# Local attention: eight masked maxima of one head each on VectorE in place of two mask products on TensorE and two maxima

## The chip, the cores and the metric

The kernel runs on one core of a Trainium2 chip. A core has TensorE (PE in the profile; PEld is its loading of weights), VectorE (DVE), ScalarE (ACT), GpSimd (POOL) and a queue for transfers (SP), each with its own stream of instructions and with semaphores between them. SBUF is the working memory of 128 partitions; PSUM has eight banks of 2 KB a partition, which TensorE writes and VectorE and ScalarE read or write. The metric is the time of one execution in microseconds; the kernel before took 3221.06 us, the median of three runs (3219.2 to 3222.68).

## The reference

Four sequences of 1024 tokens with 128 features pass six layers in turn: a gated stack `ffn0`, an attention of 16 heads, `ffn0` again, a stack `ffn1`, an ordinary causal attention, and `ffn1` again. Only `ffn1` holds the change. It has two layers, each a local attention and a gated layer. Cut to the local attention (8 heads of 64, windows of 64 tokens):

```python
q = l2norm(q) * qs
k = l2norm(k) * ksc
q, k = rotary_xpos(q, k)
bq = q.reshape(b, h, w, WINDOW, d) * QK_SCALE
bk, bv = look_around(bk), look_around(bv)          # a window sees itself and the one before
sim = jnp.einsum('bhwid,bhwjd->bhwij', bq, bk)     # 64 queries against 128 keys
mask = (i < j) | (i > j + WINDOW) | (j == -1)
sim = jnp.where(mask, -jnp.finfo(sim.dtype).max, sim)
attn = jax.nn.softmax(sim, axis=-1)
out = jnp.einsum('bhwij,bhwjd->bhwid', attn, bv)
```

So every head's scores get the same mask, the maximum of each row is taken after the mask, and the softmax is exp(score + mask - maximum), divided by its sum.

## The kernel before, in words

The data stays in SBUF as eight blocks of 512 tokens, each of four tiles of 128 tokens: 32 tiles. In an `ffn1` phase `attend` runs once for each tile and layer, 64 times, and there are two such phases: 128 tiles in all. For one tile the steps are: the projections of queries, keys and values (`project`, TensorE); sums of squares (`square` on ScalarE, `sums` on VectorE); the rotary products (`turn_a`, `turn_b` on VectorE, `add` and `normalise` on GpSimd); transposes and their copies (`turn`, `untwist`); the scores (`score`); the maxima (`top`); the exponentials with their sums (`exp`, ScalarE); the reciprocals and the division (`inverse` on VectorE, `norm_e` on GpSimd); transposes and copies of the weights (`turn_e`, `untwist_e`); the product with the values, the output projection and its addition (`weigh`, `output`, `project_out`, `collect`). VectorE also takes the statistics of other tiles (`statistics`), a Newton step for the inverse roots (`newton`) and the low half of transposed inputs (`lower`).

The scores of a tile lie in two PSUM banks (numbers 6 and 7, tag `s`), z = 0 and 1, each 128 rows (two windows of 64 queries) by four heads by 128 keys. `score` first writes the mask into both banks: one product of the identity in bf16 with the mask `lm`, 128x512, which repeats the 128x128 mask four times. The 32 products of the heads are then added to it. `top` takes, in one reduction a bank, the four maxima with their sign turned, and `exp` runs once for each of the eight heads, with this column as its bias and its row sum taken on the way. The masks, one for tiles in the middle and one for the first tile of a sequence (n = 0), are loaded by `mask` on GpSimd's queue at the start of a phase.

The order of the work isn't that of the source. Steps are recorded with a nominal time (`at`); the table `OFF` gives each step's place within a tile and `T_ATT` the pitch from tile to tile, so some five tiles are under way at a time. The planner (`Plan`) then gives every instruction a cost (`cost`), and each step its buffers, and orders all steps of the whole program over the five engines by when they must be done (`order`, `latest`; the best of six rounds). The result is one fixed order for each engine; at run time each engine takes its instructions in that order and waits on semaphores. A change of one step's cost can so move any instruction, in other phases too. Every instruction is issued through one helper, so nearly all rows of the profile carry its line, L237; they are told apart by operation, shape and tiles. The gated layers (`gated`) run in groups of four or eight blocks between the tiles.

Of `OFF`, the places that matter here:

```python
"ghi": 19.08, "sc": 19.56, "glo": 20.34, "mx0": 23.03, "mx1": 23.63, "ex03": 24.03, "ex01": 24.38, "ex00": 25.76,
"ex13": 26.10, "ex11": 26.45, "ex10": 26.79, "ex12": 27.14, "ex02": 27.48, "iv1": 28.04, "ne1": 28.53,
```

`ex03` is the exponential of bank 0, head 3: of each bank, the last head's comes first.

## Time and profile before

| | |
|---|---|
| time of the runs | 3221.06 us (3219.2 to 3222.68) |
| the profiled execution's own time | 3219.6 us |
| its span, first to last instruction | 3217.8 us |
| mean granted clock of TensorE | 0.984 |
| busy: PE, PEld | 3029.4 us (94%), 2134.7 us (66%) |
| busy: DVE, ACT, POOL | 2192.4 us (68%), 2467.9 us (77%), 1451.3 us (45%) |
| the mask products, 128x512 bf16 | 230 recorded, 383 ns each |
| the maxima, 128x4 out of 128x512 | 256, 681 ns each |
| the exponentials and others of 128x128 on ACT | 1152, 392 ns each |

The page cuts the span into 40 slices of 80 us and gives the busy share of each engine in tenths. A row of instructions gives the engine, the operation, what is written and read, partitions by elements, the count, the busy time and the mean duration of one, and then the idle time of the engine before these, with what ended it. A matmul's record includes its way through the array, so the records of products that follow each other overlap; VectorE's records overlap by some 80 ns too. What an instruction costs its engine is therefore read from one start to the next. The timeline gives start, duration, engine, operation and count of successive instructions; the table of stretches gives each engine's busy time within them. The chain of waits is followed back from the last instruction and says in whose work the time lay. A few records of products are missing from the trace.

### The profile page before, as it was taken

Reading aid. Unit: us, or ns where it says so; the run is one execution under the profiler, and the core shown is the slowest. Engines: PE = TensorE matmul, PEld = TensorE weight load, DVE = VectorE, ACT = ScalarE, POOL = GpSimd, SP = SyncE. Lnnn points to the kernel's source line nnn. Section 1 sums busy time; section 2 is a strip of 40 time slices with the busy share of each in tenths; the row PEclk is TensorE's granted clock in tenths of the full one; section 3 lists DMA queues with packets and bytes.
Section 4 is the critical chain, followed back from the end, with each engine's and each line's share of the span. In section 5 each row is a group of like instructions: output and inputs, shape, how many; then the busy total and the mean of one; then the engine's idle time right before and its main releaser. Section 6 shows DMA issues by size and latency. Waiting matters only on the chain.

```text
span 3217.8 us, 76341 instructions
## 1 busy us (share of the span) xinstructions
PE 3029.4 (94%) x27082; PEld 2134.7 (66%) x27108; DVE 2192.4 (68%) x6641; ACT 2467.9 (77%) x6856; POOL 1451.3 (45%) x1621
## 2 busy tenths in 40 slices
PE   8999999989998999899999999999999899999978
PEld 6322222567776777677777777777777677777767
DVE  8433341467867676778788778878787777676774
ACT  6999999768868687657777777767777788686873
POOL 1000000079958585523333333333343898585870
PEclk9999999999999999899999999999999999999989
DMA  1000000022212221122222222212231322222211
GB/s 40 1 1 1 1 3 11 21 68 63 57 40 58 44 56 35 42 57 49 47 55 45 46 50 45 52 44 47 54 80 34 76 54 56 44 53 49 55 42 30
DMA packets 209427, 137.31 MB, mean 43 GB/s; under 512 B 148548, under 2 KB 164632, under 8 KB 209048
## 3 DMA queue, kind: packets, MB, share of 16 engines
q1 hardware_dynamic: 208328, 131.87, 18.1%
q8 instruction: 217, 3.56, 0.5%
q14 instruction: 162, 1.33, 0.1%
q0 software_dynamic: 720, 0.56, 0.1%
HBM read 17.58 MB, written 2.10 MB: 6 GB/s over the span
## 4 chain that ended last, share of the span: by engine, by line
PE 58%; ACT 16%; DVE 13%; issue 5%; POOL 5%; DMA 1%; SPq 1%; DVEq 0%; ACTq 0%; POOLq 0%
PE wordsP L237 58%; ACT wordsS L237 12%; DVE wordsS L237 8%; POOL wordsS L237 3%; ACT words L237 3%; DVE words L237 3%; POOL words L237 1%; SPq L237 1%; DVE wordsP L237 1%; DVE wordsR L237 1%; DMA wordsS<-wordsS 1%; ACT wordsR L237 0%; DMA words<-words 0%; ACT wordsP L237 0%; DMA wordsS<-L_attn_x 0%
## 5 line engine op out<-in xcount | busy, mean ns | idle before, releaser
L237 PE MATMUL wordsP<-wordsS 128*128 128x128 f32 (+8 forms) x12062 | 1657.9, 331 | 114.2 <-POOL wordsS L237 44.1
L237 ACT ACTIVATE wordsS<-wordsP,wordsS 128x128 f32<-128x128 f32 (+4 forms) x1952 | 921.6, 495 | 335.7 <-PE wordsP L237 204.1
L237 PEld LDWEIGHTS wordsP<-wordsS 128*128 128x128 f32 (+3 forms) x10296 | 926.0, 145 | 329.4 <-POOL wordsS L237 85.3
L237 POOL TENSOR_SCALAR wordsS<-wordsS 128x128 f32<-128x128 f32 (+7 forms) x630 | 476.1, 758 | 678.6 <-DVE wordsS L237 484.5
L237 PE MATMUL wordsP<-wordsR 128*128 128x512 f32 (+2 forms) x2592 | 718.9, 409 | 13.6 <-ACT words L237 4.1
L237 POOL TENSOR_TENSOR wordsS<-wordsS 128x512 f32<-128x512 f32 (+1 forms) x512 | 532.6, 1053 | 430.2 <-DVE wordsS L237 411.4
L237 ACT COPY wordsS<-wordsP 128x512 f32<-128x512 f32 (+4 forms) x1040 | 543.8, 541 | 170.6 <-PE wordsP L237 160.7
L237 DVE TENSOR_REDUCE wordsS<-wordsP 128x1 f32<-128x512 f32 (+4 forms) x1024 | 576.9, 582 | 70.6 <-PE wordsP L237 64.1
L237 PE MATMUL wordsP<-wordsS,words 128*64 128x64 f32 (+3 forms) x6216 | 524.0, 299 | 34.6 <-DVE words L237 12.6
L237 ACT ACTIVATE wordsS<-wordsP 128x1024 f32<-128x1024 f32 (+3 forms) x646 | 516.8, 863 | 27.1 <-PE wordsP L237 22.7
L237 PEld LDWEIGHTS wordsP<-wordsR 128*128 128x128 f32 (+1 forms) x2592 | 451.1, 191 | 115.2 <-ACT words L237 10.2
L237 PE MATMUL wordsP<-words 128*128 128x512 f32 (+3 forms) x1540 | 414.7, 375 | 13.0 <-DMA words<-W_vT 10.9
L237 ACT ACTIVATION_READ_ACCUMULATOR wordsS<-wordsP,wordsS 128x1 f32 x1792 | 397.2, 222 | 0.0
L237 DVE COPY wordsS<-wordsP 128x512 f32<-128x512 f32 (+4 forms) x444 | 238.8, 551 | 219.0 <-PE wordsP L237 213.5
L237 PEld LDWEIGHTS <-wordsS 64*128 64x128 bf16 (+1 forms) x1792 | 117.7, 95 | 390.3 <-issue 373.1
L237 PEld LDWEIGHTS wordsP<-wordsS,words 128*64 128x64 f32 (+2 forms) x5704 | 302.6, 136 | 101.5 <-issue 48.1
L237 DVE TENSOR_TENSOR wordsS<-wordsP,wordsS 128x256 f32<-128x256 f32 (+3 forms) x560 | 252.7, 463 | 161.5 <-PE wordsP L237 122.8
L237 DVE TENSOR_TENSOR words<-wordsP,wordsS 128x256 f32<-128x256 f32 (+1 forms) x448 | 227.8, 527 | 133.4 <-PE wordsP L237 87.9
L237 PEld LDWEIGHTS wordsP<-words 128*128 128x128 f32 x1540 | 247.6, 192 | 44.1 <-DMA words<-W_kT 10.9
L237 PEld LDWEIGHTS wordsP<-words,wordsS 64*64 64x64 f32 (+1 forms) x4672 | 186.8, 142 | 79.4 <-issue 54.3
L237 PE MATMUL wordsP<-words,wordsS 64*64 64x128 f32 (+1 forms) x4672 | 227.3, 279 | 8.0 <-POOL words L237 3.1
L237 ACT ACTIVATE words<-wordsP,wordsS 128x512 fp32r<-128x512 f32 (+1 forms) x192 | 131.0, 689 | 69.8 <-PE wordsP L237 67.9
(62 smaller groups left out, 2219.7 us busy)
## 6 DMA issues: line engine op xcount, KB each, us to landing
words<-words SPq DMA_DIRECT2D x648, 128.0 KB
wordsS<-words SPq DMA_DIRECT2D x88, 128.0 KB
wordsS<-wordsS SPq DMA_DIRECT2D x48, 128.0 KB
wordsS<-wordsS SPq DMA_DIRECT2D x48, 112.0 KB
wordsS<-c_rot SPq DMA_DIRECT2D x16, 256.0 KB
wordsS<-L_attn_x SPq DMA_DIRECT2D x8, 256.0 KB
words<-wordsS SPq DMA_DIRECT2D x16, 128.0 KB
out_dram<-wordsS SPq DMA_DIRECT2D x8, 256.0 KB
```

Source lines behind the costliest of these rows:

```text
L237: self.follow(engine, getattr(engine.engine, name)(*args, **kw))
```

## The change

The two mask products are left out, and the heads' products now start their own sums. `top` becomes four instructions a bank, eight a tile, on VectorE: each takes one head's 128x128 scores from PSUM, adds the 128x128 mask, turns the sign, writes the result back to the same place and keeps the minimum of each row, which is the maximum with its sign turned. `exp` reads the negated scores with a scale of -1. The mask tile is 128x128 in place of 128x512.

```diff
         def mask(k):
-            W["lm", k] = tile_([128, 512], f"lm{k}", 1, BF)
-            gp.dma_start(out=W["lm", k], in_=a["c_local"][k])
+            W["lm", k] = tile_([128, 128], f"lm{k}", 1, BF)
+            gp.dma_start(out=W["lm", k], in_=a["c_local"][k][:, 0:128])
...
             def score():
                 qT, kT = V["qT", K], V["kT", K]
                 scs = V["s", K] = [plan.bank(pre + "s", [6, 7], (128, 4, 128)) for _ in range(2)]
-                for sc in scs:
-                    pe.matmul(flat(sc), self.identb, W["lm", int(n == 0)], start=True, stop=False, skip_group_check=True)
...
-                                start=False,
+                                start=True,
                                 stop=True,
                                 skip_group_check=True,
...
             def top(z):
                 if z == 0:
                     V["m", K] = tile_([128, 8], "nm", 2), tile_([128, 8], "su", 2), tile_([128, 8], "rc", 2)
-                ve.tensor_reduce(V["m", K][0][:, 4 * z : 4 * z + 4], V["s", K][z], AX.X, ALU.max, negate=True)
+
+                for c in range(4):
+                    sc = lambda: V["s", K][z][:, c, :]
+                    ve.tensor_tensor_reduce(
+                        out=sc(), in0=sc(), in1=W["lm", int(n == 0)], scale=-1.0, scalar=-NEG,
+                        op0=ALU.add, op1=ALU.min, accum_out=V["m", K][0][:, 4 * z + c : 4 * z + c + 1],
+                    )
...
                 ac.activation(
                     V["e", z, K][:, c, :], V["s", K][z][:, c, :], AF.Exp,
-                    bias=nm[:, u : u + 1], accum_out=su[:, u : u + 1],
+                    bias=nm[:, u : u + 1], scale=-1.0, accum_out=su[:, u : u + 1],
                 )
```

## The prediction

> **What bounds the kernel now.** I read the page's slices first, to find the stages that the change touches. The two local-attention phases lie at about 683 to 1348 and 2505 to 3147 us of the span; the rest holds no edited instruction.
>
> ```profile
> PE   8999999989998999899999999999999899999978
> DVE  8433341467867676778788778878787777676774
> ```
>
> There TensorE is near full and VectorE at six to eight tenths, but a slice mixes attention with gated blocks. So I asked for the stretches in which one tile's row maxima follow the next at an even pitch, and for one stretch of gated work (904 to 940):
>
> ```profile
> core 0: us, PE busy (x) PEld busy (x) DVE busy (x) ACT busy (x) POOL busy (x), PEclk, DMA share, GB/s
> 697.00:904.00 207.00, 192.82 (x2329) 149.42 (x2333) 163.19 (x514) 176.50 (x662) 188.20 (x193) 0.99 0.26 58
> 904.00:940.00 36.00, 35.67 (x264) 29.77 (x266) 14.67 (x29) 18.60 (x43) 5.72 (x7) 0.99 0.11 22
> 941.00:1081.00 140.00, 127.14 (x1517) 98.28 (x1519) 108.86 (x326) 116.47 (x440) 117.36 (x119) 0.99 0.24 53
> 1117.00:1252.00 135.00, 126.85 (x1525) 100.26 (x1526) 104.33 (x320) 116.59 (x439) 114.58 (x115) 0.97 0.26 56
> 2524.00:2731.00 207.00, 192.64 (x2326) 149.76 (x2328) 161.38 (x512) 177.29 (x663) 186.83 (x191) 0.99 0.26 58
> 2766.00:2907.00 141.00, 128.01 (x1521) 99.42 (x1522) 109.39 (x326) 116.65 (x440) 117.87 (x120) 0.98 0.24 53
> 2943.00:3080.00 137.00, 127.07 (x1525) 100.28 (x1526) 105.47 (x322) 116.25 (x439) 116.55 (x118) 0.98 0.25 55
> ```
>
> Counted by their row maxima, the six attention stretches hold 23, 15, 15, 23, 15 and 15 tiles: 106 of the 128, in 967 us, 9.12 us a tile. Busy per tile: PE 894.5/106 = 8.44, POOL 841.4/106 = 7.94, ACT 819.8/106 = 7.73, DVE 752.6/106 = 7.10. Nothing is alone at the limit; DVE is the emptiest of the four, with 2.0 us a tile to spare. In the gated stretch DVE is 41% busy and no maximum is taken.
>
> The chain of waits agrees that the load is shared. For 697 to 904:
>
> ```profile
> by line: PE wordsP L237 48.0%; POOL wordsS L237 13.4%; ACT wordsS L237 10.2%; ACT words L237 8.1%; DVE wordsS L237 6.8%; issue 5.1%; POOL words L237 2.9%; DVE wordsP L237 2.4%; DVE words L237 1.7%; ACT wordsR L237 0.6%; DVE wordsR L237 0.5%
> ```
>
> DVE holds 11% there, PE 48%. The same line for the other five stretches, in order, gives PE 15, 34, 34, 12, 26% and DVE 28, 19, 18, 26, 23%: where PE holds less, DVE and ACT hold more. Last, who waits for DVE, in the first stretch:
>
> ```profile
> POOL wordsS L237 <- DVE wordsS L237: 15.1, 15, 2.7
> ```
>
> POOL, 91% busy there (188.2 of 207), has its longest waits on DVE.
>
> **Removed from PE.** Per tile, two mask products. In the timeline of PE:
>
> ```profile
> 1123.56 0.61 PE L237 MATMUL wordsP<-wordsS 128*128 128x512 bf16 x2
> 1124.09 1.10 PE L237 MATMUL wordsP<-words,wordsS 64*64 64x128 f32 x32
> ```
>
> The scores start 0.53 us after the masks: 0.53 us a tile, 68 us over 128 tiles as PE work. What of it sets the end goes by PE's share of the chain: 0.53/8.44 = 6.3% of PE's chain time, in the six stretches 6.3, 1.3, 2.9, 4.5, 1.1 and 2.3 us, together 18 us.
>
> **Removed from DVE.** Two reductions of 128x512, each followed 0.59 us later (the next instruction starts before the recorded end):
>
> ```profile
> 797.59 0.68 DVE L237 TENSOR_REDUCE wordsS<-wordsP 128x4 f32<-128x512 f32 x1
> 798.18 0.28 DVE L237 TENSOR_TENSOR wordsS<-wordsP,wordsS 128x128 f32<-128x128 f32 x1
> ```
>
> That is 1.18 us a tile.
>
> **Added to DVE.** The built order of VectorE shows that each of the eight new instructions becomes two: the 128x128 pass and a read-out of the accumulator into a 128x1 column. It also shows a wait that the diff does not: in every group of four, the second, third and fourth pass wait for VectorE's own semaphore, which the read-out before them raises. No such pair is in the trace; the nearest rows are these, where the statistics' second half waits in the same way for the first:
>
> ```profile
> 780.32 0.28 DVE L237 TENSOR_TENSOR wordsS<-wordsP,wordsS 128x128 f32<-128x128 f32 x1
> 780.52 0.18 DVE L237 TENSOR_SCALAR wordsP<-wordsP 128x18 f32<-128x18 f32 x1
> 780.60 0.29 DVE L237 BATCH_NORM_STATS2 wordsS<-wordsS 128x6 f32<-128x128 f32 x1
> 780.93 0.18 DVE L237 BATCH_NORM_AGGREGATE wordsS<-wordsS 128x2 f32<-128x6 f32 x1
> 781.02 0.26 DVE L237 BATCH_NORM_STATS2 wordsS<-wordsS 128x6 f32<-128x128 f32 x1
> ```
>
> The pass is priced as the 128x128 tensor-tensor from PSUM: next start 0.20 us after its own. The read-out has the size of the 128x1 operations, 0.15 us, and 0.06 until an unwaited follower. A follower that waits starts 0.04 us after the end (780.60 + 0.29 = 780.89, start 780.93). So one step is 0.20 + 0.15 + 0.04 = 0.39, a group 3 x 0.39 + 0.20 + 0.06 = 1.43, a tile 2.86; net +1.68 us of DVE a tile.
>
> Bounds: if the wait and the new kind of instruction cost nothing beyond these rows, 8 x 0.26 = 2.08, net +0.90. If the read-out cannot start before the pass has ended (0.28 + 0.04 + 0.15 + 0.04 = 0.51 a step), a tile is 2 x (3 x 0.51 + 0.38) = 3.82, net +2.64. I take the middle value because ScalarE's own pairs overlap in that way:
>
> ```profile
> 781.20 0.37 ACT L237 ACTIVATE wordsS<-wordsP,wordsS 128x128 f32<-128x128 f32 x1
> 781.45 0.21 ACT L237 ACTIVATION_READ_ACCUMULATOR wordsS<-wordsP,wordsS 128x1 f32 x1
> ```
>
> The read-out starts 0.25 us into a pass of 0.37.
>
> A rule speaks against my step. The Trainium skill, "VectorE: DVE Perf Modes", section "The DRAIN you can't avoid", says that a semaphore after each VectorE instruction costs nothing, since the pipeline empties anyway. By it the eight would cost the 2.08 us of the lower bound. The rows above disagree: the waited start is 0.04 us after the end, the unwaited one 0.08 to 0.09 us before it.
>
> **Latency.** The first exponential of a group is that of its last head in every tile (OFF has ex03 and ex13 first, and the built order keeps 3, 1, 0, 2). So it waits for the fourth pass, and no exponential starts early: from scores to first exponential a group goes from 0.68 to about 1.5 us, while the scores themselves come 0.53 us sooner. The two score banks are held about as long as before. On DVE's queue stand behind the eight: the rotary products (POOL's adds wait for them), the Newton step, the statistics, the split of the transposed inputs (PE's projections wait) and the reciprocals.
>
> **At nothing.** The mask loads (four on POOL's queue, 0.53 to 0.75 us each to issue) shrink to a quarter and stand well ahead of the first scores; were they late, a load lands in 3 to 5.4 us, once a phase. The 256 identity weight loads run beside products. The exponentials keep their count and shape with a constant scale. The planner orders all queues anew, outside these phases too; I give that no sign.
>
> **The sum.** DVE's need becomes 7.10 + 1.68 = 8.78 us of a 9.12 us tile: from the emptiest engine to the fullest (PE falls to 7.91). Two readings. By the chain: DVE's chain time grows by 1.68/7.10 = 23.7% (5.6+9.2+6.0+8.8+8.7+7.6 = 46 us by its shares above) less PE's 18 us: +28 us. By load: the fullest engine off PE is POOL at 91%; DVE at 91% needs 8.78/0.91 = 9.65 us a tile, +0.53 x 106 = +56 us. The chain reading does not see that DVE gains share as it fills, the load reading ignores that PE gives way; I take the middle, +0.40 us a tile, 42 us, and half that rate for the other 22 tiles (fill, drain, about gated blocks), 4 us. Together +46 us on the profiled execution's 3219.6 us: 3266. The median of the runs is 1.5 us above that one: **3267 us**. Its own range: +30 to +62, 3250 to 3285.
>
> **Rivals.**
> - *Faster: DVE's extra fits its idle time and PE's relief arrives.* For it: DVE has 2.0 us a tile free, +1.68 fits, and the longest stretches sit on PE (48 and 34%). Against: the free time lies in waits, and POOL waits for DVE already. With DVE wholly hidden the gain is 18 us in the six stretches, 22 over all tiles: 3200. It decides below the lower bound's step: at 0.26 us the chain gives 46 x 0.90/1.68 = +25 against -18, so DVE must also be off the chain for half its time. Chance 0.14.
> - *A draw.* The step is near 0.26 us, gain and loss meet, and what is left is the new order: 3214 to 3245. Chance 0.10, 0.06 of it within the bound of a measurement, about 0.2% (3214.6 to 3227.5).
> - *Dearer: the read-out waits for the pass, or the new kind of pass has a longer start.* Step 0.51, net +2.64: by chain 72 - 18 = +54, by load (9.74/0.91 - 9.12) x 106 = +168, middle +111: 3333, reaching 3380. For it: no row shows this kind of pass. Chance 0.16.
>
> **How the numbers follow.** Forecast 0.60, the rivals 0.14, 0.10, 0.16. Slower by over 0.2%: 0.60 + 0.16 + 0.04 = 0.80; within 0.06; faster 0.14. The range leaves half of the faster case and the top of the dearer one out: 3203 to 3340.
>
> **What would show it.** In the changed profile: 1024 passes and 1024 read-outs on DVE, the passes starting 0.39 us apart within a group (0.26 or 0.51 for the others); no 128x512 bf16 product in these phases; DVE busy over 8.5 us a tile and above 90% of the attention stretches, PE below 8.1; a pitch near 9.5 us, with gated stretches and both first attentions unchanged within a few us; and more waits on DVE by POOL and ACT. I am wrong if DVE stays below 85%, if the pitch keeps to 9.1 us, or if the time changes in the untouched stages.

## The result, and the profile after

The changed kernel takes 3322.21 us (median of four runs, 3319.05 to 3330.73) against 3220.13 us for the kernel before on the same chip (four runs, 3217.0 to 3222.68): a ratio of 1.032, 95% interval 1.030 to 1.034. It is 102 us slower; the forecast was 46 us slower. The profiled execution took 3321.1 us, its span 3319.1 us, at a mean granted clock of 0.974 (before 3219.6, 3217.8 and 0.984).

The slices of the changed kernel's page, in the order PE, DVE:

```profile
PE   7999999988888889799999999999998888889878
DVE  8433341588868688778788778877777897786875
```

VectorE's digits in the two local-attention phases (slices 9 to 17 and 32 to 39) are mostly 7 and 8 where they were mostly 6 and 7, TensorE's mostly 8 where they were mostly 9. The table of stretches, between the same tiles' maxima as before (the six steady ones; the second line is the gated stretch between the first two):

```profile
core 0: us, PE busy (x) PEld busy (x) DVE busy (x) ACT busy (x) POOL busy (x), PEclk, DMA share, GB/s
699.50:921.10 221.60, 190.59 (x2287) 151.33 (x2287) 191.19 (x838) 177.71 (x662) 188.44 (x192) 0.98 0.25 55
921.10:961.80 40.70, 37.51 (x270) 31.35 (x271) 16.90 (x45) 18.68 (x43) 7.22 (x9) 0.95 0.11 23
961.80:1109.50 147.70, 124.68 (x1486) 99.45 (x1484) 126.85 (x535) 115.61 (x438) 116.18 (x118) 0.96 0.23 51
1149.90:1295.20 145.30, 125.08 (x1503) 101.62 (x1504) 122.89 (x527) 115.34 (x437) 113.28 (x114) 0.96 0.24 52
2583.30:2802.10 218.80, 188.74 (x2283) 150.19 (x2283) 190.48 (x834) 176.30 (x659) 187.34 (x191) 0.99 0.24 55
2840.70:2987.80 147.10, 123.41 (x1485) 98.74 (x1484) 126.91 (x535) 115.42 (x438) 116.54 (x118) 0.96 0.23 51
3028.40:3176.00 147.60, 125.70 (x1497) 101.65 (x1497) 124.10 (x529) 115.08 (x436) 114.90 (x115) 0.96 0.22 49
```

The same 106 tiles now take 1028 us, 9.70 us a tile in place of 9.12. Busy per tile: PE 8.29, DVE 8.32, POOL 7.89, ACT 7.69. So VectorE went from the emptiest engine to the fullest, but it is only 86% busy (8.32 of 9.70): no engine is full.

One group of passes on VectorE, in the timeline:

```profile
786.69 0.27 DVE L237 CUSTOM_DVE_ANT_0 wordsP<-wordsP,wordsS 128x128 f32<-128x128 f32 x1
786.88 0.14 DVE L237 DVE_READ_ACCUMULATOR2_ANT wordsS<- 128x1 f32 x1
787.06 0.30 DVE L237 CUSTOM_DVE_ANT_0 wordsP<-wordsP,wordsS 128x128 f32<-128x128 f32 x1
787.28 0.14 DVE L237 DVE_READ_ACCUMULATOR2_ANT wordsS<- 128x1 f32 x1
787.45 0.30 DVE L237 CUSTOM_DVE_ANT_0 wordsP<-wordsP,wordsS 128x128 f32<-128x128 f32 x1
```

A read-out starts 0.21 us after its pass on average and lasts 0.14; the next pass starts 0.03 to 0.04 us after the read-out's end. From pass to pass it is 0.392 us in the median (380 to 393 ns for nine in ten), and a group takes 1.52 us from the first start to the last end. TensorE's timeline has the scores directly behind other work, with no mask product in front:

```profile
1155.97 2.34 PE L237 MATMUL wordsP<-wordsR 128*128 128x512 f32 x9
1158.24 1.10 PE L237 MATMUL wordsP<-words,wordsS 64*64 64x128 f32 x32
```

The chain of waits from 699.5 to 921.1:

```profile
by line: DVE wordsP L237 18.8%; PE wordsP L237 18.4%; DVE wordsS L237 17.1%; ACT wordsS L237 15.4%; DVE words L237 7.9%; ACT words L237 7.8%; issue 5.2%; POOL wordsS L237 2.8%; DVE wordsR L237 1.8%; POOL words L237 1.6%; SPq L237 1.3%; DMA 
```

VectorE holds 46% of this stretch, where it held 11%; its largest part, "DVE wordsP", contains the passes, whose output is in PSUM. Over all six stretches, by the same line of each, its share of the chain went from 20% to 40%. And the longest waits in the first stretch, as who waits for whom, us in total, times and the longest one; first after, then before:

```profile
PEld wordsP L237 <- POOL wordsS L237: 21.0, 26, 2.4
POOL wordsS L237 <- DVE wordsS L237: 18.5, 13, 3.1
...
ACT wordsS L237 <- DVE wordsS L237: 12.8, 14, 1.7
```

```profile
PEld wordsP L237 <- POOL wordsS L237: 10.2, 19, 1.6
...
ACT wordsS L237 <- DVE wordsS L237: 2.1, 3, 1.0
```

POOL's waits for VectorE went from 15.1 to 18.5 us, ScalarE's from 2.1 to 12.8, and TensorE's weight loads wait 21.0 us for POOL in place of 10.2.

Added up from the two traces, the 101 us between the spans lie here: six steady stretches +62 us (966 to 1028); the six gated gaps between and behind them +21 (200 to 221); the stretch from the last tile of the first phase to the first of the second, where nothing is edited, +13 (1158 to 1171); fill and drain of the two phases +6.

### The profile page after: what moved, and what is told of

Read it like the earlier page. It is cut to its first block, busy times and chain, and to the rows that moved or that the text cites. A ratio compares the mean times of both kernels' runs of the same rounds, so it can differ in the third digit from the quotient of the medians.

```text
span 3319.1 us, 77684 instructions
## 1 busy us (share of the span) xinstructions
PE 3024.7 (91%) x26852; PEld 2151.7 (65%) x26852; DVE 2354.4 (71%) x8433; ACT 2471.5 (74%) x6856; POOL 1454.1 (44%) x1621
## 4 chain that ended last, share of the span: by engine, by line
PE 52%; DVE 21%; ACT 14%; issue 6%; POOL 5%; DMA 1%; SPq 1%; DVEq 0%; ACTq 0%; POOLq 0%
PE wordsP L237 52%; ACT wordsS L237 11%; DVE wordsS L237 10%; DVE wordsP L237 6%; DVE words L237 4%; POOL wordsS L237 3%; ACT words L237 3%; POOL words L237 1%; SPq L237 1%; DVE wordsR L237 1%; DMA wordsS<-wordsS 0%; ACT wordsR L237 0%; DMA words<-W_vT 0%; DMA words<-L_ffn_b 0%; ACT wordsP L237 0%
## 5 line engine op out<-in xcount | busy, mean ns | idle before, releaser
L237 PE MATMUL wordsP<-wordsS 128*64 128x256 f32 (+6 forms) x11832 | 1599.2, 331 | 183.4 <-POOL wordsS L237 88.6
L237 PEld LDWEIGHTS wordsP<-wordsS 128*128 128x128 f32 (+3 forms) x10296 | 936.1, 146 | 427.0 <-POOL wordsS L237 138.2
L237 PE MATMUL wordsP<-wordsR 128*128 128x512 f32 (+2 forms) x2592 | 729.4, 413 | 22.8 <-DVE wordsS L237 10.3
L237 DVE TENSOR_REDUCE wordsS<-wordsP 128x1 f32<-128x512 f32 (+3 forms) x768 | 403.7, 549 | 58.1 <-PE wordsP L237 52.3
L237 PE MATMUL wordsP<-words 128*128 128x512 f32 (+3 forms) x1540 | 417.6, 376 | 15.1 <-DMA words<-W_vT 11.6
L237 DVE CUSTOM_DVE_ANT_0 wordsP<-wordsP,wordsS 128x128 f32<-128x128 f32 x1024 | 303.6, 297 | 36.2 <-PE wordsP L237 9.9
L237 PEld LDWEIGHTS <-wordsS 64*128 64x128 bf16 (+1 forms) x1536 | 100.7, 94 | 344.9 <-issue 330.3
L237 PE MATMUL wordsP<-words,wordsS 64*64 64x128 f32 (+1 forms) x4672 | 243.5, 283 | 31.8 <-ACT wordsS L237 18.7
L237 PEld LDWEIGHTS wordsP<-words,wordsS 64*64 64x64 f32 (+1 forms) x4672 | 197.4, 144 | 88.3 <-ACT wordsS L237 41.9
```

Of the source, the lines that this page charges most:

```text
L237: self.follow(engine, getattr(engine.engine, name)(*args, **kw))
```

## The experiments

The theory that I began with was the prediction's: VectorE's added time makes it a shared bound (load). Its rivals: the wait between the passes, which delays the last maximum of each group (lateness); the score banks, held until the exponentials have read them (hold); writing back into the PSUM bank, for what it does besides the wait (place); and the planner, which counts a group at 1.17 us where it takes 1.52 (plan). "Pitch" is the length of a steady tile, over the same 106 tiles. Ratios are to the kernel before, run on the same chip, with the 95% interval.

### The place that the passes write to, and the wait between them

The passes write to an SBUF tile in place of their own PSUM bank, and the exponentials read that tile in place. In the built order no pass then waits for VectorE's own semaphore.

```diff
+                V["e", z, K] = tile_([128, 4, 128], "e", 4)
...
-                        out=sc(), in0=sc(), in1=W["lm", int(n == 0)], scale=-1.0, scalar=-NEG,
+                        out=V["e", z, K][:, c, :], in0=V["s", K][z][:, c, :], in1=W["lm", int(n == 0)], scale=-1.0, scalar=-NEG,
...
-                    V["e", z, K][:, c, :], V["s", K][z][:, c, :], AF.Exp,
+                    V["e", z, K][:, c, :], V["e", z, K][:, c, :], AF.Exp,
```

> The kernel after, but each of the eight passes writes its negated scores to SBUF (the tile that the exponentials fill) and not back to PSUM. The built order then has no wait of a pass on VectorE's own semaphore. Load theory (the loss is VectorE filling up by the step of 0.39 us): the step falls to about 0.26 us, VectorE's work to about 8.0 us a tile, and most of the 102 us goes: 3225 to 3260 us. Rival (the loss is the later maxima and the new order, not the load): the last head's maximum comes 0.4 us sooner, little else: 3285 to 3320 us. A third thing can spoil it: ScalarE reading SBUF in place of PSUM.

Measured: 3235.09 us, 1.0042 (1.0029 to 1.0055); pitch 9.11 us, VectorE 7.49 us a tile. A group in its timeline:

```profile
788.58 0.26 DVE L237 CUSTOM_DVE_ANT_0 wordsS<-wordsP,wordsS 128x128 f32<-128x128 f32 x1
788.76 0.08 DVE L237 DVE_READ_ACCUMULATOR2_ANT wordsS<- 128x1 f32 x1
788.76 0.28 DVE L237 CUSTOM_DVE_ANT_0 wordsS<-wordsP,wordsS 128x128 f32<-128x128 f32 x1
788.98 0.08 DVE L237 DVE_READ_ACCUMULATOR2_ANT wordsS<- 128x1 f32 x1
788.98 0.28 DVE L237 CUSTOM_DVE_ANT_0 wordsS<-wordsP,wordsS 128x128 f32<-128x128 f32 x1
```

The next pass starts with the read-out of the one before it: 0.211 us a step (median) in place of 0.392, 0.92 us a group in place of 1.52. The same eight passes on the same scores now cost 14 us (0.0042 of 3220); the other 90 us (1.0322 less 1.0042) hang on where they write. That changes more than the wait, though: the bank is free sooner too. So the next kernel keeps the banks held: it writes the passes to SBUF as above, but its exponentials read the unmasked scores in PSUM with their old scale, and so leave the mask out of the exponentials.

```diff
-                    V["e", z, K][:, c, :], V["e", z, K][:, c, :], AF.Exp,
-                    bias=nm[:, u : u + 1], scale=-1.0, accum_out=su[:, u : u + 1],
+                    V["e", z, K][:, c, :], V["s", K][z][:, c, :], AF.Exp,
+                    bias=nm[:, u : u + 1], accum_out=su[:, u : u + 1],
```

> As the kernel with negated scores in SBUF (3235 us), but the exponentials read the unmasked scores in PSUM (the mask is left out of the exponentials, so what they compute is not the reference). No self-waits, VectorE's work as there, but the two score banks are held until the last exponential, as in the kernel after. If the hold of the banks is what the SBUF form saved: 3270 to 3300 us. If it was VectorE's work and waits alone: 3225 to 3245 us.

Measured: 3236.38 us, 1.0058 (1.0043 to 1.0073), pitch 9.25 us, VectorE 7.55. Held banks cost next to nothing by themselves in the total (1 us, 5 by the ratios), though the steady tile is 0.14 us longer than in the SBUF kernel. Last, the SBUF kernel with the planner's cost of a pass lowered to 0.17 us, so that its order is another one:

```diff
+            if name == "tensor_tensor_reduce":
+                return 0.17
```

> The kernel with negated scores in SBUF, with the planner told 0.17 us a pass (1.04 us a group, where it took 1.17 and the chip 1.05). Only the order changes: 3220 to 3240 us. Below 3215 us it would beat both kernels.

Measured: 3230.57 us, 1.0039 (1.0025 to 1.0053), pitch 9.13. Three kernels without the wait, each with another order, lie within 6 us of each other and some 85 to 92 us below the changed kernel. Their pitch is 9.11 to 9.25 us; the changed kernel and two more below that keep the wait in other orders (with the mask products put back, and with another planned cost) have 9.70 to 9.73. So it is shown that passes written back into their bank cost this, and that it isn't an accident of one order.

That it is by the wait is argued, not shown alone. In place a pass differs from one into SBUF in three ways: it waits; its read-out takes 141 ns and not 83; and where it hardly waits, in the alternating kernel below, a step still takes 0.249 us and not 0.211. Of the 0.18 us between 0.392 and 0.211, some 0.14 are so the wait and 0.04 the place. Other work isn't slowed by the writing: in the steady stretches of the changed kernel an exponential takes 392 ns (398 in the held-bank kernel), GpSimd's operation on two 128x512 tiles 1080 (1079), VectorE's on 128x256 417 (419). But no run takes the wait alone away and gains by it: the alternating kernel, which comes near, is the slowest of all. How 0.18 us a step can come to so much is the question of the next two sections.

### VectorE's load: part of it, and not by a ceiling

The kernel before, with a reduction of 768 elements that serves nothing behind each maximum (0.86 us):

```diff
+                x = tile_([128, 8], "xx", 2)
+                ve.tensor_reduce(x[:, 0:6], self.ident.unsqueeze(1).broadcast_to([128, 6, 128]), AX.X, ALU.max)
```

> The kernel before, with one more reduction on VectorE behind each maximum (768 elements of a constant tile, some 0.87 us), for which no exponential waits. Masks stay on TensorE. Load theory: VectorE gets as full as in the kernel after (about 8.8 us a tile) without the later maxima and without TensorE's relief: 3310 to 3350 us. Latency rival: nothing on the chain waits for it: 3220 to 3260 us.

Measured: 3296.51 us, 1.0229 (1.0214 to 1.0244), pitch 9.74, VectorE 8.68 us a tile (89%). Load does cost time: 1.7 us a tile made the tile 0.62 us longer. Some of that is lateness, since the reduction behind the first maximum delays the second, which ended 4.03 us after the scores in place of 3.31 (means over the steady tiles). But at the fill of the changed kernel it costs far less. The SBUF kernel with a reduction of 384 elements behind each group of passes:

```diff
                         op0=ALU.add, op1=ALU.min, accum_out=V["m", K][0][:, 4 * z + c : 4 * z + c + 1],
                     )
+                x = tile_([128, 8], "xx", 2)
+                ve.tensor_reduce(x[:, 0:3], self.ident.unsqueeze(1).broadcast_to([128, 3, 128]), AX.X, ALU.max)
```

> The kernel with negated scores in SBUF (3235 us: no self-waits, and the banks free after the passes), with one more reduction on VectorE behind each group of passes (384 elements of a constant tile, about 0.46 us), for which no exponential waits. VectorE is then about as full as in the kernel after. Load theory: the loss comes back, 3295 to 3325 us. Bank theory: the banks are free early whatever VectorE does, 3235 to 3260 us.

Measured: 3242.37 us, 1.0075 (1.0059 to 1.0090), pitch 9.26. Its first two steady stretches:

```profile
core 0: us, PE busy (x) PEld busy (x) DVE busy (x) ACT busy (x) POOL busy (x), PEclk, DMA share, GB/s
698.70:910.50 211.80, 187.74 (x2291) 149.49 (x2290) 191.30 (x882) 182.44 (x665) 189.13 (x194) 0.98 0.26 57
947.90:1088.90 141.00, 123.01 (x1477) 98.40 (x1475) 123.95 (x555) 120.58 (x436) 113.91 (x116) 0.95 0.24 53
```

VectorE has 191.3 us of work in the first stretch, the changed kernel's 191.2, and the stretch is 10 us shorter. In the six stretches VectorE is 89% busy (8.25 of 9.26), more than the changed kernel's 86%, and holds about 28% of the chain, not 40%. The same load on the kernel with held banks (mask left out of the exponentials as there):

```diff
+                x = tile_([128, 8], "xx", 2)
+                ve.tensor_reduce(x[:, 0:3], self.ident.unsqueeze(1).broadcast_to([128, 3, 128]), AX.X, ALU.max)
```

> As the one before, with the added reduction of 0.46 us behind each group of passes, so that VectorE is about as full as in the kernel after and the banks are held as there (the mask is left out of the exponentials here too). With banks free early this load cost 7 us. If load costs only where the banks are held: 3300 to 3325 us, near the kernel after. If load and hold simply add: 7 us over the run before. If neither matters without the self-waits: under 3260 us.

Measured: 3263.76 us, 1.0137 (1.0122 to 1.0152), pitch 9.35, VectorE 8.32. So 0.93 us a tile of load behind the maxima costs 11 us on the SBUF kernel (by the ratios) or 25 us on the held-bank kernel, out of 85 to 90, and here too some of it is lateness of the second group (its last maximum ended 4.84 us after the scores, without the load 4.13). A VectorE that is as full as the changed kernel's doesn't make its time.

### Lateness: the same load ahead of the maxima

The cleanest comparison moves one reduction. The kernel with the load of 768 elements, now ahead of the maximum:

```diff
+                x = tile_([128, 8], "xx", 2)
+                ve.tensor_reduce(x[:, 0:6], self.ident.unsqueeze(1).broadcast_to([128, 6, 128]), AX.X, ALU.max)
                 ve.tensor_reduce(V["m", K][0][:, 4 * z : 4 * z + 4], V["s", K][z], AX.X, ALU.max, negate=True)
-                x = tile_([128, 8], "xx", 2)
-                ve.tensor_reduce(x[:, 0:6], self.ident.unsqueeze(1).broadcast_to([128, 6, 128]), AX.X, ALU.max)
```

> As the kernel before with the added reduction of 0.87 us (3297 us), but the added one stands ahead of the maximum, so that the maximum and the exponentials come later by it. Same work on every engine. Load theory: 3290 to 3305 us as before. Bank theory: the banks are held 0.9 to 1.7 us longer a tile, 3330 to 3400 us.

Measured: 3320.94 us, 1.0320 (1.0305 to 1.0336), pitch 9.93 against 9.74. The same move in the SBUF kernel with 384 elements:

```diff
+                x = tile_([128, 8], "xx", 2)
+                ve.tensor_reduce(x[:, 0:3], self.ident.unsqueeze(1).broadcast_to([128, 3, 128]), AX.X, ALU.max)
                 for c in range(4):
                     ve.tensor_tensor_reduce(
...
-                x = tile_([128, 8], "xx", 2)
-                ve.tensor_reduce(x[:, 0:3], self.ident.unsqueeze(1).broadcast_to([128, 3, 128]), AX.X, ALU.max)
```

> The passes written into SBUF, with the reduction of 384 elements (0.465 us) of each group AHEAD of its four passes in place of behind them (3242): the same instructions and the same planned cost, only the place differs. Lateness theory: the maxima of each group come some 0.46 us later, so 3280 to 3320, pitch 9.5 to 9.9 us a tile. Rival, how full VectorE is decides, or the plan's cost: the place is indifferent, 3235 to 3260, pitch 9.2 to 9.35.

Measured: 3258.67 us, 1.0123 (1.0107 to 1.0139), pitch 9.42 against 9.26, which lies between what the two theories asked for. Its timeline and its first two stretches:

```profile
788.78 0.54 DVE L237 TENSOR_REDUCE wordsS<-wordsS 128x3 f32<-128x384 f32 x1
789.24 0.28 DVE L237 CUSTOM_DVE_ANT_0 wordsS<-wordsP,wordsS 128x128 f32<-128x128 f32 x1
```

```profile
core 0: us, PE busy (x) PEld busy (x) DVE busy (x) ACT busy (x) POOL busy (x), PEclk, DMA share, GB/s
699.70:913.80 214.10, 188.15 (x2289) 149.93 (x2289) 192.06 (x880) 182.00 (x664) 189.10 (x193) 0.98 0.26 57
951.30:1095.00 143.70, 124.44 (x1475) 98.75 (x1475) 124.29 (x556) 121.85 (x437) 114.05 (x115) 0.95 0.24 52
```

In both pairs of built programs the order of TensorE, ScalarE, GpSimd and SyncE is the same, instruction for instruction, and VectorE has the same instructions: only the place of one kind differs. The busy times agree, the stretches don't (214.1 against 211.8, 143.7 against 141.0). A reduction of 0.46 us costs 15 us more ahead of the maxima than behind them (0.0048 of 3220), one of 0.86 us 29 us (0.0091): in both pairs some 33 us for each microsecond. Read from the traces as the time from the scores' end, the last maxima came 0.51 and 0.76 us later, by which it is 30 and 39. So lateness costs time with nothing else changed.

By this rate, an estimate for the wait: three steps that are 0.18 us longer put the last maximum of the first group 0.55 us later and, one group behind the other, that of the second 1.09; 0.82 us on average, 27 us. They also take 1.09 us of VectorE a tile, which by the two load pairs (11 and 25 us for 0.93) is 13 to 29 us. Together 40 to 56 us. In the steady stretches the changed kernel is 48 us longer than the held-bank kernel without the wait (1028 against 980), so there the two could make up what is seen. The price of the load holds some lateness itself, so the sum counts a part of that twice.

I also tried to make the lateness without the wait, by small reductions of 104 elements (0.17 us) between the passes of a group, so that the passes stand 0.38 us apart. On the SBUF kernel:

```diff
+                x = tile_([128, 8], "xx", 2)
                 for c in range(4):
...
+                    if c < 3:
+                        ve.tensor_reduce(x[:, c : c + 1], self.ident[:, 0:104], AX.X, ALU.max)
```

> The kernel with negated scores in SBUF (3235 us), with a small reduction of a constant tile (some 0.17 us) between the passes of a group, so that they are 0.39 us apart as in the kernel after. The banks are free after the passes. If VectorE's time for the passes is what costs, held banks or not: 3290 to 3320 us. If it costs only where the banks are held until the exponentials: 3240 to 3265 us.

Measured: 3309.46 us, 1.0272 (1.0257 to 1.0287), pitch 9.84. And on the kernel with held banks (mask left out of the exponentials):

```diff
+                x = tile_([128, 8], "xx", 2)
                 for c in range(4):
...
+                    if c < 3:
+                        ve.tensor_reduce(x[:, c : c + 1], self.ident[:, 0:104], AX.X, ALU.max)
```

> The same spaced passes in the form whose exponentials read the unmasked scores in PSUM (the mask is left out of the exponentials), so that the banks are held to the end as in the kernel after: it is the kernel after in timing, without writing in place. If stall and hold together make the loss: 3290 to 3325 us. If writing in place had a cost of its own: under 3275 us.

Measured: 3314.38 us, 1.0286 (1.0267 to 1.0305), pitch 9.69. Both came out as lateness asked, but they have a flaw: the planner adds 0.12 us between instructions and so counts such a group at 2.05 us, where it takes 1.35 (three steps of 0.38 and one of 0.21). With its costs corrected:

```diff
+            if name == "tensor_tensor_reduce":
+                return 0.12
+            if name == "tensor_reduce" and free_size(out) == 1:
+                return 0.055
             if name in ("tensor_reduce", "bn_stats"):
```

> The kernel with the passes kept apart by small reductions (passes written into SBUF, a reduction of 104 elements between two passes), with the plan told 0.12 us for a pass and 0.055 us for a small reduction, so that a group is planned at about 1.35 us, which is what it takes, and not at about 2.05. Lateness theory (a group's last maximum comes 0.43 us later because the passes are 0.38 us apart): 3290 to 3315, pitch 9.6 to 9.9 us a tile, as with the plan uncorrected (3309). Rival, the plan charged the seven instructions of a group too much and spread the tile by itself: 3240 to 3260, pitch 9.1 to 9.3.

Measured: 3290.33 us, 1.0221 (1.0203 to 1.0239), pitch 9.31. By the pitch the rival was right: most of the length of the spaced tiles was the plan's doing. (The second condition also lowers the cost of the maxima of the gated stretches and of the other attention; the stretch between the phases became 28 us longer than in the SBUF kernel, 1195 against 1167, and the total says little.) What spacing leaves is 0.20 us a tile over the SBUF kernel, with some load in it, half of what the estimate would give there. And its last maxima come about as late as the changed kernel's (2.96 and 5.49 us after the scores for the two groups, against 3.05 and 5.15), while its tile is 0.39 us shorter. So the spaced runs prove nothing of lateness; the two pairs with equal orders do, and the size of its share in the changed kernel stays an estimate, with orders alone able to move a tile by some tenths of a microsecond.

### TensorE's relief

The kernel before without the two mask products, and with nothing in their place: the mask is left out of the scores.

```diff
-                for sc in scs:
-                    pe.matmul(flat(sc), self.identb, W["lm", int(n == 0)], start=True, stop=False, skip_group_check=True)
...
-                                start=False,
+                                start=True,
```

> The kernel before without the two mask products (the mask is left out of the computation; maxima and exponentials as they were). It is TensorE's relief alone. By the share of the chain it is worth 18 to 22 us: about 3200 us. If the four engines are coupled tightly enough that TensorE's relief goes into waits: 3212 to 3222 us. If TensorE is the bound where its share is 48%: 3185 us or less.

Measured: 3203.76 us, 0.9946 (0.9929 to 0.9963): a gain of 17 us, 0.13 us a steady tile. Then the changed kernel with the mask products put back beside the passes, so that the mask is added twice (its tile is 128x512 again):

```diff
+                for sc in scs:
+                    pe.matmul(flat(sc), self.identb, W["lm", int(n == 0)], start=True, stop=False, skip_group_check=True)
...
-                                start=True,
+                                start=False,
```

> The kernel after with the two mask products on TensorE as well (the mask is then added twice, which changes nothing of the softmax). Load theory: TensorE has 1.4 us a tile to spare behind a full VectorE, so its relief of 0.53 us was worth little there: 3322 to 3335 us. If gain and loss simply add, as the chain reading took it: 3340 to 3360 us.

Measured: 3311.57 us, 1.0276 (1.0260 to 1.0291): 15 us faster than the change with TensorE relieved. In the steady stretches the two are alike (9.73 and 9.70 us); the gain lies outside them, in the gated gaps (206 against 221 us) and between the phases (1161 against 1171). The relief was worth 17 us in the kernel before, whose chain lies 30% on TensorE and 20% on VectorE in the steady stretches, and nothing in the tiles of the changed kernel, where it lies 19% and 40% on them.

### The plan, and the time outside the edited steps

The changed kernel with the planner's cost of a pass at 0.27 us, so that it counts a group at 1.44 us and not at 1.17:

```diff
+            if name == "tensor_tensor_reduce":
+                return 0.27
```

> The kernel after, with the planner told what a pass and its read-out cost (0.27 us and 0.12 between them, 1.44 us a group, where it took 1.17). Only the order changes. If the loss comes from an order made for too cheap a step: 3255 to 3290 us. Load theory and bank theory (the two score banks are held from the first score to the last exponential, 9.47 of the 9.70 us pitch) both leave it near the kernel after: 3305 to 3325 us.

Measured: 3303.51 us, 1.0264 (1.0249 to 1.0280): 19 us back, and none of it in the steady tile (9.72). The gated gaps are 210 in place of 221 us, the stretch between the phases 1161 in place of 1171. So about half of the time lost outside the steady tiles comes with an order that is made for shorter passes. One way in which time is lost where no pass runs is seen at the end of the first steady stretch. Stretches of 3.4 us of the changed kernel there:

```profile
core 0: us, PE busy (x) PEld busy (x) DVE busy (x) ACT busy (x) POOL busy (x), PEclk, DMA share, GB/s
911.40:914.80 3.40, 3.40 (x45) 2.86 (x44) 3.16 (x21) 2.78 (x14) 1.73 (x2) 1.00 0.00 0
914.80:918.20 3.40, 0.45 (x2) 0.01 (x1) 2.67 (x8) 2.87 (x12) 1.27 (x1) 1.00 0.42 95
918.20:921.60 3.40, 2.90 (x34) 2.44 (x35) 2.63 (x12) 0.93 (x6) 3.16 (x3) 0.51 0.13 28
921.60:925.00 3.40, 3.40 (x9) 2.46 (x8) 3.09 (x16) 2.11 (x3) 2.97 (x5) 0.50 0.00 0
925.00:928.40 3.40, 3.40 (x16) 2.56 (x15) 1.50 (x2) 1.72 (x3) 0.00 (x0) 0.99 0.00 0
```

TensorE stands still for most of one stretch, and its granted clock is half for the next two. Its timeline gives the wait and what runs slowly behind it:

```profile
918.70 2.33 PE L237 MATMUL wordsP<-words,wordsS 64*64 64x128 f32 x32 [3.45 <-ACT wordsS L237]
920.96 0.47 PE L237 MATMUL wordsP<-wordsS,words 128*128 128x128 f32 x1
921.09 7.63 PE L237 MATMUL wordsP<-wordsR 128*114 128x512 f32 x24
```

The same 24 gated products in the kernel before, where TensorE had stood for 2.05 us:

```profile
901.14 0.94 PE L237 MATMUL wordsP<-wordsS 128*128 128x512 bf16 x2 [2.05 <-ACT wordsS L237]
...
904.05 6.12 PE L237 MATMUL wordsP<-wordsR 128*114 128x512 f32 x24
```

They take 6.1 us there and 7.6 here: a longer wait of the last tile reaches into the gated work behind it. Over the span, drops to half went from 18 to 30, and the time lost by them from 52 to 88 us. How much of the 40 us outside the steady tiles is due to this and how much to the order itself was not separated: a wait for a late tile costs time with or without a lower clock.

The exponentials of the changed kernel in the order of the heads, so that the first of a group could start behind the first pass:

```diff
-    "ghi": 19.08, "sc": 19.56, "glo": 20.34, "mx0": 23.03, "mx1": 23.63, "ex03": 24.03, "ex01": 24.38, "ex00": 25.76,
-    "ex13": 26.10, "ex11": 26.45, "ex10": 26.79, "ex12": 27.14, "ex02": 27.48, "iv1": 28.04, "ne1": 28.53,
+    "ghi": 19.08, "sc": 19.56, "glo": 20.34, "mx0": 23.03, "mx1": 23.63, "ex00": 24.03, "ex01": 24.38, "ex02": 25.76,
+    "ex10": 26.10, "ex11": 26.45, "ex12": 26.79, "ex13": 27.14, "ex03": 27.48, "iv1": 28.04, "ne1": 28.53,
```

> The kernel after, with the exponentials of a bank in the order of heads 0, 1, 2, 3 in place of 3, 1, 0, 2, so that the first one waits for the first pass and not for the fourth. VectorE's work is the same. Load theory: 3312 to 3330 us. Bank theory: the exponentials can follow the passes, a bank is held up to 1.2 us less, and the pitch falls by 0.3 to 0.6 us: 3255 to 3290 us.

Measured: 3321.64 us, 1.0316 (1.0299 to 1.0333), no difference. From the first pass's start to the first exponential it is 1.77 us on average, as in the changed kernel (1.76). The two built programs differ only in the heads that 768 of the 1024 exponentials take; every wait is the same, and the first exponential of each tile waits for all four passes of a group, though it reads one head. So the early start never came to be, and whether it would help stays open.

### Two other arrangements

Half of the change: bank 0 as before (mask product and one reduction), bank 1 by four passes into SBUF.

```diff
-                for sc in scs:
-                    pe.matmul(flat(sc), self.identb, W["lm", int(n == 0)], start=True, stop=False, skip_group_check=True)
+                pe.matmul(flat(scs[0]), self.identb, W["lm", int(n == 0)], start=True, stop=False, skip_group_check=True)
...
+                if z:
+                    V["e", z, K] = tile_([128, 4, 128], "e", 4)
+                    for c in range(4):
+                        ve.tensor_tensor_reduce(
+                            out=V["e", z, K][:, c, :], in0=V["s", K][z][:, c, :], in1=W["lm", int(n == 0)][:, 0:128], scale=-1.0,
+                            scalar=-NEG, op0=ALU.add, op1=ALU.min, accum_out=V["m", K][0][:, 4 * z + c : 4 * z + c + 1],
+                        )
+                    return
                 ve.tensor_reduce(V["m", K][0][:, 4 * z : 4 * z + 4], V["s", K][z], AX.X, ALU.max, negate=True)
...
```

The rest of the edit lets bank 1's products start their own sums, and its exponentials read the negated scores from SBUF with a scale of -1.

> Bank 0 as in the kernel before (mask product, one reduction), bank 1 by four passes into SBUF. TensorE gives back half of its relief (0.27 us a tile), VectorE takes 0.45 us a tile in place of 0.9. If the pitch is set by the fullest of four coupled engines, the mixture balances them: 3205 to 3220 us. If loss goes by dose: half-way between 3221 and 3235 us, 3225 to 3232 us.

Measured: 3183.73 us (3180.97 to 3184.54), 0.9888 (0.9872 to 0.9905): 36 us faster than the kernel before, the fastest here. Pitch 8.83. Its first steady stretch:

```profile
core 0: us, PE busy (x) PEld busy (x) DVE busy (x) ACT busy (x) POOL busy (x), PEclk, DMA share, GB/s
700.10:904.60 204.50, 184.83 (x2277) 148.38 (x2291) 166.98 (x674) 176.77 (x660) 184.82 (x189) 0.99 0.26 58
```

Over the six stretches a tile has 8.05 us of TensorE (before 8.44), 7.32 of VectorE, 7.83 of ScalarE and 7.82 of GpSimd. With another planned cost of a pass, 0.17 us, and so another order:

```diff
+            if name == "tensor_tensor_reduce":
+                return 0.17
```

> The mixture (bank 0 with mask product and reduction, bank 1 with four passes into SBUF; 3184 us), with the planner told 0.17 us a pass. Only the order changes: 3178 to 3190 us.

Measured: 3187.28 us, 0.9892 (0.9876 to 0.9909), pitch 8.84. So the gain does not hang on one order. Why this mixture beats both the kernel before and all passes into SBUF is not shown.

The other arrangement keeps the passes in PSUM and takes the stall out: all eight passes of a tile in one step, alternating between the banks, so that each waits for the pass two places before it.

```diff
                 for c in range(4):
+                    for y in range(2):
-                    sc = lambda: V["s", K][z][:, c, :]
+                        sc = lambda: V["s", K][y][:, c, :]
...
-                o(f"mx{z}", top, z)
+                if z == 0:
+                    o("mx0", top, 0)
```

> The kernel after, with the eight passes of a tile taken in turn from the two banks (head 0 of bank 0, head 0 of bank 1, head 1 of bank 0, and so on). Each still writes in place and waits on VectorE's own semaphore, but for the pass two before it, which is long done. If the stall between passes (0.39 us from start to start, against 0.21 in SBUF) is what costs: the step falls to about 0.22 us and the time to 3235 to 3270 us. If writing in place, or holding the banks, costs by itself: 3295 us or more.

Measured: 3343.53 us, 1.0381 (1.0362 to 1.0400), the slowest, although a step fell to 0.249 us (median) and VectorE's work to 7.84 us a tile; pitch 10.22. This time VectorE has less to do and the tile is longer. Lateness of the maxima doesn't explain it: the last ones of the two banks ended 2.82 and 3.07 us after the scores, against 3.05 and 5.15 in the changed kernel. By what was expected ahead, the run speaks for a cost of writing in place, or of holding the banks, besides the wait; but the held-bank kernel shows little of the second, and this edit also makes one step of two, eight passes without a break, and another order. Which of these made it slow stays open.

## Why the prediction was wrong

- **The step of the passes: right.** 0.39 us was worked out, 0.392 measured, and the three terms as well: 0.21 to the read-out (0.20 taken), 0.14 for it (0.15), 0.03 to 0.04 for the waited start (0.04). The wait is there, as the built order showed.
- **The rule against it: wrong here.** By the Trainium skill, "VectorE: DVE Perf Modes", section "The DRAIN you can't avoid", a semaphore after each instruction costs nothing; the page measured it on eight copies in a row, and says itself that an instruction which isn't held back starts earlier. Here a step in place takes 0.392 us with the wait and 0.249 where it hardly waits (0.211 into SBUF): the wait costs some 0.14 us on each of the six passes of a tile that have it.
- **The steady tile: direction right, the size too small.** The forecast took the middle of two readings, +0.40 us a tile, 42 us; measured +0.58, 62 us. The load reading alone had +0.53. But its reason, VectorE at a ceiling of 91%, is not what happened: VectorE is at 86%, and a kernel with the same work on VectorE behind the maxima stands at 9.26 us a tile. The load reading came near by luck, counting the waits as work. That the waits cost more than their work because they bring the maxima late is the estimate above, not shown for this kernel.
- **TensorE's relief of 18 us: no gain in this kernel.** The term that made the chain reading +28 and not +46 was priced by TensorE's share of the chain before. It is right for the kernel before (17 us without the mask products), but the change itself moved the chain to VectorE, and with the products put back the steady tile is 9.73 us in place of 9.70. Without this term the middle would have been 51 us and not 42; measured were 62.
- **"The two score banks are held about as long as before": wrong.** From the start of the scores to the end of the last exponential the mean over the 106 tiles went from 8.31 to 9.47 us, and what lies between that end and the next tile's scores shrank from 0.79 to 0.28 us. What the longer hold costs by itself is little, as the held-bank kernel showed. The scores' earlier start of 0.53 us did not pay for 1.6 us more between the first maximum's start and the last one's end (1.96 to 3.57).
- **The rest at 4 us: the largest error.** The forecast gave the 22 other tiles half the rate, the planner's new order no sign, and held the gated stretches and the other attentions for unchanged. Measured: +40 us, 21 in the gated gaps, 13 between the phases, 6 in fill and drain. This is 36 of the 55 us by which the forecast missed; 20 are the steady tile. Telling the planner the passes' length brings 19 us of the 40 back, so the term that was put at nothing for the new order was worth about that; the cause of the other 21 stays open, with the lower clock in the gated gaps as a part that was not measured alone.
- **The rivals.** "Dearer" ends near the measured time (3333), but for a step of 0.51 us, which isn't there. Of "faster", what may hold is that TensorE's relief pays if VectorE's extra stays small: the half change fits that and takes 3184 us, less than the 3200 worked out.
- **The signs named ahead.** Passes 0.39 us apart, no 128x512 mask product, more waits of POOL and ScalarE on VectorE: as said. VectorE over 8.5 us a tile and above 90%: 8.32 and 86%. TensorE below 8.1: 8.29, with more of it at half clock. Gated stretches unchanged: no, which the forecast had named as a way to be wrong.

## What to carry to other kernels

An instruction that stands between a product and its consumer is priced by when its last result comes, and not only by how long it occupies its engine: here, with the order kept, each microsecond by which a tile's maxima came late cost 30 to 39 us over 128 tiles, while 0.93 us a tile of other work behind them cost 11 to 25 us in all. Neither count decides across different orders: the alternating kernel had less work on VectorE and earlier maxima, and the longest tile. Look in the built order for waits of an engine on itself, and try another place for the output before giving up an instruction: the same passes written to SBUF, for one bank of the two, turned a loss of 3.2% into a gain of 1.1%. And where a planner orders the whole program, a new instruction's real duration has to be put in its table, and the stretches that the change does not touch have to be in the sum.

## What the runs showed of the hardware

- The masked maximum with an accumulator is two instructions on VectorE, a pass (recorded with 284 ns into SBUF, 297 in place with the wait, 331 in the alternating kernel) and a read-out. Where the next pass doesn't wait for it, it starts together with the read-out: 0.211 us after the pass before with the output in SBUF, 0.249 in the alternating kernel with the output in PSUM. The read-out's record is 83 ns in the first case and 141 in the second; it is 141 as well where the next pass waits, so it goes by the place of the output and not by the wait.
- Whether the waits are there is decided by the place of the output: in place in the PSUM bank each pass waits for the read-out before it, into SBUF none does. It is the program that has the wait; that the chip would need it was not tried.
- TensorE's granted clock fell to half in units of 3.4 us, and each drop (18 before, 30 after) follows a window of that length in which TensorE was idle for 1.67 us or more, half of it. The Trainium skill, "TensorE: Matmul & The Clock Gate", section "Part 1: The HAM clock gate (the "warmup" mystery)", tells of the half clock after an idle window of about 3.4 us; these traces show it after windows that were only partly idle. Not every such window has a drop behind it: among others, one of 1.69 us idle in the kernel before and one of 1.76 us in the changed kernel had none. A drop, behind the window from 897.6 to 901.0 us of the kernel before:

```profile
core 0: us, PE busy (x) PEld busy (x) DVE busy (x) ACT busy (x) POOL busy (x), PEclk, DMA share, GB/s
897.60:901.00 3.40, 1.49 (x7) 0.97 (x6) 2.42 (x6) 2.80 (x12) 1.89 (x2) 1.00 0.37 82
901.00:904.40 3.40, 3.26 (x36) 2.16 (x36) 2.99 (x12) 0.59 (x4) 2.85 (x3) 0.54 0.15 34
```
